# Filter taps of a convolution by distances, two images or four in one operation

## The chip, the cores and the metric

The kernel runs on one core of a Trainium2 chip. The core's engines take part side by side, each with its own instruction stream: TensorE (PE in the profile; its weight loads are shown as PEld) multiplies matrices into PSUM, VectorE (DVE) and ScalarE (ACT) do elementwise work, GpSimd (POOL) does little here, and SyncE (SP) issues most DMAs. The metric is the time of one execution in device microseconds; lower is better.

## The reference, cut to what matters

Sixteen images of 128 channels and 28 x 28 places go through four layers. Layer 0, which the change touches, is an "adder" convolution: each output is minus a sum of absolute differences over channels and nine taps, not a sum of products.

```python
x = x + L0(group_norm(x))     # L0: -sum over 128 channels, 9 taps of |w - x|; 128 filters, 3x3, zero padding
x = L1(x)                     # two 3x3 convolutions with 4-bit weights, batch norm, quantized
t = tokens(x)                 # 784 tokens of 128 channels per image
t = t + additive_attention(ln(t))   # scores[i, j] = v . tanh(Wi[i] + Wi[j]), softmax over j
t = t + mixture_of_experts(ln(t))   # 8 experts, the best 2 per token
t = t + linear_attention(ln(t))
t = t + spectral(ln(t))             # 16 causal filters as products with banded matrices, and more
```

Everything is float32.

## The kernel before, in words

**Layer 0 as taps.** `|w - x|` is made in one of two ways. Kind "a": ScalarE writes `|w - x|` in one activation (line 1351). Kind "m": VectorE writes `max(x, w)` (line 1353), since `|w - x| = 2 max(x, w) - x - w`; a second tap of kind "m" may be added onto the first in the same tile (line 1355, `max(x, w) + part`). Each such tile, 128 channels by two images, holds one tap, or two merged ones, of one filter. TensorE then sums it over the channels: the weights are a block of 32 columns that is zero but for one column of -1 or -2 (`sel`, shifted so that the column falls on the filter's row), and the matmul adds into that filter's row of a PSUM accumulator (line 1335). A matmul with 32 weight columns uses one of TensorE's four column groups. The parts `-x` and `-w` of kind "m", and what taps outside the image bring, are added by `plain_taps` (one small product per pair) and as a bias `sw`.

**Tiling.** The images go in eight pairs. A pair has its input in `pad`, rows of the two images alternating, with a border of zeros. Each of the four column groups has its quarter of the filters, 32, and a list of the tiles of these filters in order; a `Plan` says which taps are kind "a", kind "m", or merged ("m45" are taps 4 and 5 in one tile). One step (`streams`) takes the next tile of each of the four lists, shifted against each other by `turns`, so that a step mixes both kinds: four tiles, then 16 matmuls (four tiles by four PSUM banks of 14 interleaved rows, 392 columns). Pair 0 has the plan ALONE (264 steps), pair 1 SECOND (256), pairs 2 to 7 BESIDE (208 each, 6.5 tiles per filter).

**Order around it.** All else is interleaved with these steps by hand. In step n (loop at line 1360) the code emits, in this order: `rows` (score units: four tanh of 394 columns on ScalarE, line 917, whose products for TensorE wait in `products`, line 901); `taps_of(n + 1)`; the next elementwise parts of the lanes (`ahead`); `sums(n)`, the step's 16 matmuls; the products; the next TensorE parts of the lanes (`behind`). The lanes are generators that yield `EV` before elementwise work and `PE` before TensorE work: `plain` (plain_taps), `convs` (group norm of the next pair and the quantized convolutions of the last, line 542), `conv_out` (the spectral layer: per job three 128-wide matmuls u at line 1232, a copy on ScalarE at line 1242, one 128-wide product into out at line 1235, and band and mat fetches on SP's queue at lines 1179 and 1181, two jobs ahead), and `chain` (the token layers). A rate per lane says how many parts a step takes. TensorE keeps the order as emitted; the other engines' orders are a scheduler's.

**Buffers.** Tap tiles rotate through a ring of ten, shared with other short-lived tiles (`slot`); in pair 0 there are more places. At a pair's end the convolutions must be through, `pad` is rewritten (line 488), and VectorE adds accumulators, bias and the pair's input into `x1p` (line 1385, eight operations of 196 columns). After pair 7 comes the tail: score units that are left (in a form with the adds on VectorE, line 910, and one tanh for four rows, line 912), the rest of the chain and the spectral layer.

Of the kernel before, what the change touches and what calls it, by code (L numbers as in the profile page):

```python
# [20 lines left out]
TAPS = [(dy, dx) for dy in range(3) for dx in range(3)]  # L21


class Plan:
# [5 lines left out]
    def __init__(self, kinds, tiles_of, turns, maxima):  # L30
        self.kinds, self.tiles_of, self.turns, self.maxima = kinds, tiles_of, turns, maxima

    def streams(self):


        quarters = []
        for j, turn in enumerate(self.turns):
            mine = [(m, *x) for m in range(32) for x in self.tiles_of(m, j)]
            quarters.append(mine[turn:] + mine[:turn])
        return list(zip(*quarters))  # L40

    def cut(self, kind):


        of = {}
        for j in range(4):
            for m in range(32):
                for x, taps in self.tiles_of(m, j):
                    for k, region in zip(taps, regions(taps)):
                        if x == kind and region != WHOLE:  # L50
                            of.setdefault(k, set()).add(32 * j + m)
        return {k: frozenset(f) for k, f in of.items()}
# [7 lines left out]
def maxima(all_, **some):  # L60
    return [(int(k), "all") for k in all_] + [(int(k), of) for of, taps in some.items() for k in taps]

FOUR, OTHER = tiles("a0 m4 a2 m5 a6 m7 a8 m13"), tiles("a0 m4 m1 a2 m5 m3 a6 m7 m8")
ALONE = Plan("alone", lambda m, j: OTHER if (m + j) % 4 == 3 else FOUR, (0, 2, 5, 7), maxima("13457", fourth="8"))

EARLY = 6
TWO, ONE = tiles("m13 a0 m4 m5 m6 a2 m7 m8"), tiles("m13 a0 m4 m5 m6 m2 m7 m8")
SECOND = Plan("second", lambda m, j: FOUR if m < EARLY else ONE if (m - EARLY) % 2 else TWO, (0, 2, 5, 7),  # L70
              maxima("13457", late="68", late_odd="2"))

SIX, SEVEN = tiles("m13 a0 m45 m6 a2 m78"), tiles("m13 a0 m7 m45 a2 m8 m6")
BESIDE = Plan("beside", lambda m, j: SEVEN if (m + j) % 4 > 1 else SIX, (0, 2, 4, 5), maxima("1345786"))
CONV_TAPS = [1, 2, 3, 4, 5, 6, 7]


def reach(k):

    dy, dx = TAPS[k]  # L80
    return 2 * (dy == 0), 2 * HW - 2 * (dy == 2), int(dx == 0), HW - (dx == 2)


WHOLE = reach(4)


def regions(taps):


    first = reach(taps[0])  # L90
    for k in taps[1:]:
        r = reach(k)
        if r[0] < first[0] or r[1] > first[1] or r[2] < first[2] or r[3] > first[3]:
            first = WHOLE
    return [first] + [reach(k) for k in taps[1:]]
# [19 lines left out]
RING, ROWS = 10, 14  # L115


RATE_X, RATE_Y, RATE_S, RATE_C, RATE_A, RATE_0, RATE_T, RATE_Z = 1.2, 0.93, 2.0, 1.0, 1.5, 0.9, 2.0, 0.75
# [89 lines left out]
def kernel(ctx: ExitStack, tc: tile.TileContext, a: dict, out: bass.AP):  # L208
# [5 lines left out]
    ring = ctx.enter_context(tc.tile_pool(name="ring", bufs=RING))  # L214
# [6 lines left out]
    NP = B // 2  # L221


    stage = {"pair": 0, "prepared": False, "alone": False}
    turns = {"psx": 0, "psu": 0, "row": 0, "tap": 0}
# [20 lines left out]
    def tap_slot(name):  # L246
        places = []
        if stage["pair"] == 0:
            places = [rows_in[:, 4 * WIN * k : 4 * WIN * k + 2 * T] for k in range(ROWS // 4)]
            if stage["prepared"]:  # L250
                places += [spare(2 * T) for _ in range(4)]
        k = turns["tap"] = (turns["tap"] + 1) % (RING + len(places))
        return places[k] if k < len(places) else slot(2 * T, name)

    def slot(n, name):
        return ring.tile([P, 4 * WIN], F32, tag="d", name=name)[:, :n]
# [6 lines left out]
    def load_pair(p, name):  # L263
        t = slot(2 * T, name).rearrange("p (b t) -> p b t", b=2)
        nc.sync.dma_start(t, a["x"][2 * p : 2 * p + 2].rearrange("b c t -> c b t"))
        return t
# [10 lines left out]
    x0 = load_pair(0, "x0")  # L277
# [34 lines left out]
    pad = const.tile([P, PR, PC], F32, name="pad")  # L312
    x1p = const.tile([P, PR, PC], F32, name="x1p")
    q1p = const.tile([P, PR, PC], F32, name="q1p")
    for t in (pad, x1p, q1p):
        nc.vector.memset(t, 0.0)


    masks = one.tile([P, NE, P], F32, tag="dg", name="masks")
    nc.vector.memset(masks[:, :3], 0.0)  # L320
    fourth, late, late_odd = (masks[:, i, :] for i in range(3))
    for j in range(4):
        nc.vector.memset(fourth[:, 32 * j + 3 - j : 32 * j + 32 : 4], 1.0)
        nc.vector.memset(late[:, 32 * j + EARLY : 32 * j + 32], 1.0)
        nc.vector.memset(late_odd[:, 32 * j + EARLY + 1 : 32 * j + 32 : 2], 1.0)
    filters = {"all": ones, "fourth": fourth, "late": late, "late_odd": late_odd}

    sw = {}
    for plan in (ALONE, SECOND, BESIDE):
        wsum = one.tile([P, P], F32, tag="gate", name=f"wsum_{plan.kinds}")  # L330
        part = one.tile([P, P], F32, tag="gt", name=f"part_{plan.kinds}")
        nc.vector.memset(wsum, 0.0)
        for k, of in plan.maxima:
            nc.vector.tensor_tensor(part, w0[:, k, :], filters[of], ALU.mult)
            nc.vector.tensor_tensor(wsum, wsum, part, ALU.add)
        q = ps("sw_ps")
        nc.tensor.matmul(q[:, :1], wsum, ones[:, :1], start=True, stop=True)
        sw[plan.kinds] = const.tile([P, 1], F32, name=f"sw_{plan.kinds}")
        nc.vector.tensor_copy(sw[plan.kinds], q[:, :1])

    taken = {}
    NB = len(TAPS)
    for plan in (ALONE, SECOND, BESIDE):
        taken[plan.kinds] = const.tile([NB + len(plan.maxima), P], F32, name=f"taken_{plan.kinds}")
        for i, (_, of) in enumerate(plan.maxima):
            nc.sync.dma_start(taken[plan.kinds][NB + i : NB + i + 1, :], filters[of][:1, :])
    channel_sums = scratch.tile([PR, PC], F32, name="channel_sums")
# [3 lines left out]
    row_sets = slot(12 * P, "row_sets")  # L351

    def row_of(fs):

        if fs not in sets:
            t = sets[fs] = blk(row_sets, len(sets) - 1)
            nc.vector.memset(t[:1], 0.0)
            for j in range(4):
                left = sorted(f - 32 * j for f in fs if f // 32 == j)
                while left:  # L360
                    runs = [[m for m in range(left[0], 32, step)] for step in (1, 2, 4)]
                    runs = [r[: next((i for i, m in enumerate(r) if m not in left), len(r))] for r in runs]
                    run = max(runs, key=len)
                    step = run[1] - run[0] if len(run) > 1 else 1
                    nc.vector.memset(t[:1, 32 * j + run[0] : 32 * j + run[-1] + 1 : step], 1.0)
                    left = [m for m in left if m not in run]
# [161 lines left out]
    def quantized_convs(p):  # L528
        yield EV
        lv = None  # L530
        for i, name, src in ((0, "L1_conv_w1", x1p), (1, "L1_conv_w2", q1p)):
            w = slot(9 * P, f"{name}_{p}").rearrange("p (k f) -> p k f", f=P)
            nc.sync.dma_start(w, wq[name].rearrange("p (k f) -> p k f", f=P))
            if i == 0:
                yield EV
# [894 lines left out]
```

## Time and profile before

| what | value |
|---|---|
| time, median of 3 runs | 11,595.7 us (11,589.33 to 11,598.8) |
| the profiled execution's own time | 11,592.63 us |
| its span | 11,590.9 us |
| busy: PE, DVE, ACT | 10,973.1, 10,499.6, 10,074.4 us |
| tap operations on DVE: L1353, L1355 | 4,493.8 and 3,720.7 us |
| tap operations on ACT: L1351 | 3,233.6 us |
| tanh of scores on ACT: L917 | 5,285.5 us |
| tap matmuls on PE: L1335, both kinds | 5,056.6 and 4,176.8 us |
| mean granted TensorE clock | 0.986 |
| DMA | 393.14 MB, q1 at 11.9% of the 16 engines |

Busy time of PE is the union of matmul records; matmuls overlap, so it says when something was in flight and not how much of PE was used. In a row of an operation, the count after x is followed by its busy time and the mean duration of one in ns, then by the idle time of the engine before it and what ended it. A window's row has, for each engine, busy time and number of instructions, then the TensorE clock, the DMA share and GB/s. The pads' rewrites start at 859, 2,038, 3,332, 4,654, 5,982, 7,328 and 8,665 us, and the last tap matmul ends at 9,992 us; these are the ends of the stages.

### The profile page before, as it was taken

To read this page: it belongs to the slowest core of one execution; us is meant where nothing else is said; L and a number is where in the kernel's file an instruction comes from. 1 tells how busy PE (TensorE), PEld (TensorE's weight loads), DVE (VectorE), ACT (ScalarE), POOL (GpSimd) and SP (SyncE) were. 2 spreads that over 40 slices of the span, in tenths; PEclk is the share of its full clock that TensorE was granted. 3 is DMA by queue.
4 is the path that set the end of the run, shared out by engine and by line. 5 is a ranking of instruction groups with operands and counts; after the bars stand their busy time and mean duration, and the time that the engine had idled before them with its cause. 6 is when DMAs were issued, how large, how long until landed. Compare 5 with 4: busy or idle time off the path is not lost.

```text
span 11590.9 us, 236925 instructions
## 1 busy us (share of the span) xinstructions
PE 10973.1 (95%) x97914; PEld 6520.6 (56%) x97914; DVE 10499.6 (91%) x15188; ACT 10074.4 (87%) x14557; POOL 173.3 (1%) x145
## 2 busy tenths in 40 slices
PE   7999999999999999999999999999999999999999
PEld 5554655565555655555555555565555655444446
DVE  9998899999999999999999899999999999999981
ACT  7887998979989898898988989899798998988872
POOL 0000000000000000000000000000000000000000
PEclk9999999999999999999999999999999999999999
DMA  1210000010110111011010110111110111121224
GB/s 31 62 38 4 1 3 10 17 39 23 38 31 24 39 28 42 19 32 38 26 39 22 33 37 25 30 33 33 37 30 20 36 34 38 33 57 52 57 59 108
DMA packets 417672, 393.14 MB, mean 34 GB/s; under 512 B 48297, under 2 KB 402945, under 8 KB 416338
## 3 DMA queue, kind: packets, MB, share of 16 engines
q1 hardware_dynamic: 416162, 376.23, 11.9%
q8 instruction: 771, 12.63, 0.5%
q14 instruction: 307, 2.51, 0.1%
q10 hardware_dynamic: 432, 1.77, 0.0%
HBM read 359.86 MB, written 17.94 MB: 33 GB/s over the span
## 4 chain that ended last, share of the span: by engine, by line
PE 54%; DVE 20%; ACT 18%; issue 2%; POOL 0%; DMA 0%; ACTq 0%; DVEq 0%; POOLq 0%; SPq 0%
PE acc L1335 22%; ACT rows_in L917 11%; PE sp L901 10%; PE u L1232 10%; DVE d L1353 7%; DVE d L1355 7%; ACT d L1351 5%; PE out L1235 4%; PE conv_ps L542 2%; DVE th L910 2%; PE ex L1070 1%; PE av L985 1%; ACT th L912 1%; DVE mx L961 1%; DVE sc L974 1%
## 5 line engine op out<-in xcount | busy, mean ns | idle before, releaser
L917 ACT ACTIVATE rows_in<-wi 128x394 f32<-128x394 f32 x9872 | 5285.5, 628 | 197.9 <-PE sp L901 191.3
L1335 PE MATMUL acc<-d,sel_m 128*32 128x392 f32 (+3 forms) x37224 | 5056.6, 493 | 127.3 <-DVE d L1355 119.4
L1353 DVE TENSOR_SCALAR d<-pad,w 128x1458 f32<-128x1458 f32 (+2 forms) x4653 | 4493.8, 1005 | 317.4 <-PE acc L1335 312.5
L1335 PE MATMUL acc<-d,sel_a 128*32 128x378 f32 (+1 forms) x17136 | 4176.8, 479 | 70.2 <-ACT d L1351 69.1
L1355 DVE SCALAR_TENSOR_TENSOR d<-pad,w,d 128x1512 f32<-128x1512 f32 (+1 forms) x2113 | 3720.7, 1778 | 8.5
L1351 ACT ACTIVATE d<-pad,w 128x1458 f32<-128x1458 f32 x2142 | 3233.6, 1537 | 372.3 <-PE acc L1335 365.3
L1335 PEld LDWEIGHTS acc<-d,sel_m 128*32 128x32 f32 x37224 | 1927.5, 111 | 927.3 <-issue 419.6
L901 PE MATMUL sp<-rows_in,vz 128*32 128x394 f32 x19744 | 2275.8, 496 | 0.8 <-ACT rows_in L917 0.8
L1335 PEld LDWEIGHTS acc<-d,sel_a 128*32 128x32 f32 x17136 | 1380.7, 111 | 1097.9 <-issue 292.4
L1232 PE MATMUL u<-band,up 128*128 128x392 f32 (+2 forms) x6144 | 1626.7, 401 | 19.1 <-ACT us L1242 15.9
L1232 PEld LDWEIGHTS u<-band,up 128*128 128x128 f32 x6144 | 1093.1, 190 | 958.6 <-issue 243.1
L901 PEld LDWEIGHTS sp<-rows_in,vz 128*32 128x32 f32 x19744 | 1270.6, 110 | 475.1 <-ACT rows_in L917 107.2
L912 ACT ACTIVATE th<-th 128x1576 f32<-128x1576 f32 x668 | 980.5, 1529 | 110.3 <-DVE th L910 104.0
L910 DVE TENSOR_SCALAR th<-wi 128x394 f32<-128x394 f32 x2672 | 933.6, 422 | 3.4 <-PE sp L901 2.7
L901 PE MATMUL sp<-th,vz 128*32 128x394 f32 x5344 | 532.1, 506 | 75.0 <-ACT th L912 73.9
L1235 PE MATMUL out<-us,mat 128*128 128x392 f32 (+1 forms) x1408 | 580.4, 494 | 0.1
L1242 ACT COPY us<-u 128x392 f32<-128x392 f32 x704 | 337.3, 479 | 235.0 <-PE u L1232 233.2
L1242 ACT COPY rows_in<-u 128x392 f32<-128x392 f32 x320 | 154.3, 482 | 280.1 <-PE u L1232 279.4
L1074 DVE SCALAR_TENSOR_TENSOR t<-ex,gate,t 128x128 f32<-128x128 f32 x896 | 309.1, 347 | 51.7 <-PE ex L1070 45.0
L901 PEld LDWEIGHTS sp<-th,vz 128*32 128x32 f32 x5344 | 132.7, 109 | 367.1 <-ACT th L912 202.5
L1070 PE MATMUL ex<-ew,xt 128*128 128x512 f32 x448 | 235.9, 610 | 41.1 <-DVE t L1074 37.7
L1235 PE MATMUL out<-rows_in,mat 128*128 128x392 f32 (+1 forms) x640 | 261.3, 493 | 0.0
(318 smaller groups left out, 5947.8 us busy)
## 6 DMA issues: line engine op xcount, KB each, us to landing
band<-band SPq DMA_DIRECT2D x1024, 196.0 KB
mat<-mats SPq DMA_DIRECT2D x1024, 64.0 KB
lags<-lag_mats SPq DMA_DIRECT2D x80, 192.0 KB
L_conv_w<-q_L_conv_w SPq DMA_DIRECT2D x16, 576.0 KB
ew<-in_L_ffn_expert_w_dram SPq DMA_DIRECT2D x16, 512.0 KB
eb<-eb_rows SPq DMA_DIRECT2D x16, 448.0 KB
x<-in_x_dram SPq DMA_DIRECT2D x8, 784.0 KB
band<-band_out SPq DMA_DIRECT2D x32, 196.0 KB
```

The costliest lines, as they stand in the source:

```text
L901: nc.tensor.matmul(sp[32 * j : 32 * j + 32, lo : lo + WIN], vz[:, 32 - m : 64 - m], rows[j], start=m == 0, stop=m == Q - 1, skip_group_che ...
L910: nc.vector.tensor_scalar(th[:, j, :], wi[:, i + Q * j : i + Q * j + WIN], wi[:, i + Q * j : i + Q * j + 1], None, ALU.add)
L912: nc.scalar.activation(th, th, AF.Tanh)
L917: nc.scalar.activation(rows[j], wi[:, i + Q * j : i + Q * j + WIN], AF.Tanh, bias=wi[:, i + Q * j : i + Q * j + 1])
L1070: nc.tensor.matmul(q, blk(xt, i), ew[:, 4 * h : 4 * h + 4, :], start=True, stop=True)
L1232: nc.tensor.matmul(q[:, P * i : TH], up[:, to ^ odd, i, :], t[:, :w], start=i == 0, stop=i == 2)
L1235: nc.tensor.matmul(acc[:, lag:TH], m0, u[:, : TH - lag], start=False, stop=n is None and not copied)
L1242: nc.scalar.copy(u[:, :TH], q[:, :TH])
L1335: nc.tensor.matmul(acc[:, lo - 14 * c : hi - 14 * c, c0:c1], sel[kind][:, 31 - m : 63 - m], d[:, lo:hi, c0:c1], start=n == 0, stop=n == le ...
L1351: nc.scalar.activation(part, x, AF.Abs, bias=wk, scale=-1.0)
L1353: nc.vector.tensor_scalar(part, x, wk, None, ALU.max)
L1355: nc.vector.scalar_tensor_tensor(part, x, wk, part, ALU.max, ALU.add)
```

## The change

The images are taken in five groups: images 0-1, then 2-5, 6-9, 10-13 (four at a time), then 14-15. A tap tile of a group of four is 128 channels by four images, and one operation writes it. TensorE's four column groups become the four images: a tile's eight matmuls (four images by two PSUM banks of 14 rows) all use the same weights. With four images, an accumulator of two banks holds 32 filters, so a group goes through the filters in four phases; groups of two images take two tiles per step and two phases. Accumulators exist twice and phases take turns. The input has no border now; taps only write the places that they reach, and merged taps are chosen so that the first covers the second. At a phase's end ScalarE adds the bias and writes the sums to DRAM (`x1s`), and the quantized convolutions read them back with the input. Plans per group are new, tap operations are emitted two (half as large) steps ahead and not one, rates are per group, and the ring of ten tiles becomes ten half tiles with explicit owners (`take`, `free`; `lend` for other users, four at most). `ROWS` goes from 14 to 12.

```diff
+class Group:
+    def __init__(self, first, n, plan, rows, pace):
+        self.first, self.n, self.plan, self.rows, self.pace = first, n, plan, rows, pace
+        self.tall = n * HW
+    def firsts(self, phase):
+        return [P // self.n * phase + 32 * (j // self.n) for j in range(4)]
+    def streams(self, phase):
+        lists = []
+        for f0 in self.firsts(phase)[:: self.n]:
+            mine = [(f0 + m, *x) for m in range(32) for x in self.plan.tiles_of(f0 + m)]
+            turn = self.plan.turn if lists else 0
+            lists.append(mine[turn:] + mine[:turn])
+        return list(zip(*lists, strict=True))
...
-SIX, SEVEN = tiles("m13 a0 m45 m6 a2 m78"), tiles("m13 a0 m7 m45 a2 m8 m6")
-BESIDE = Plan("beside", lambda m, j: SEVEN if (m + j) % 4 > 1 else SIX, (0, 2, 4, 5), maxima("1345786"))
+FOUR, OTHER = tiles("a0 m4 a2 m5 a1 m7 a8 m36"), tiles("a0 m4 m1 a2 m5 m3 a6 m7 m8")
+ALONE = Plan("alone", lambda f: OTHER if (f + f // 32) % 4 == 3 else FOUR, 5)
+SEVEN, EIGHT = tiles("a0 m45 a2 m1 a6 m78 m3"), tiles("a0 m4 a2 m5 m1 a6 m78 m3")
+EARLY = Plan("early", lambda f: EIGHT if f % 2 else SEVEN)
+TWO, THREE = tiles("a0 m45 m1 a2 m78 m6 m3"), tiles("a0 m45 m1 m36 m2 m78")
+BESIDE = Plan("beside", lambda f: THREE if f % 4 == 3 else TWO)
+ONE, NONE = tiles("a0 m45 m1 m78 m2 m36"), tiles("m0 m45 m1 m78 m2 m6 m3")
+LATE = Plan("late", lambda f: NONE if (f + f // 32) % 2 else ONE, 3)
+GROUPS = (Group(0, 2, ALONE, 0.0, 1.0), Group(2, 4, EARLY, 0.85, 0.9), Group(6, 4, BESIDE, 1.95, 1.0),
+          Group(10, 4, BESIDE, 1.95, 1.0), Group(14, 2, LATE, 3.2, 1.6))
...
-RING, ROWS = 10, 14
+HALVES, HALF, ROWS = 10, 2 * T, 12
+AHEAD = 2
+STEP = 208
...
+    def tap_sums_out(g, phase, accs):
+        s = take(1)
+        if s is None:
+            return False
+        t = s.ap[:, :T]
+        for c in range(2):
+            nc.scalar.activation(t[:, c * NCK : (c + 1) * NCK], accs[c][:, :NCK], AF.Identity,
+                                 bias=sw[g.plan.name][:, phase : phase + 1])
+        for j, f0 in enumerate(g.firsts(phase)):
+            nc.sync.dma_start(x1s[g][j % g.n, f0 : f0 + 32, :], t[32 * j : 32 * j + 32])
+        s.free()
+        return True
...
-    def quantized_convs(p):
+    def quantized_convs(g, p):
+        held = None
+        while held is None:
+            yield EV
+            held = lend(2)
+        first, raw = (held.ap[:, i * HALF : (i + 1) * HALF].rearrange("p (b t) -> p b t", b=2) for i in range(2))
+        lo = 2 * p - g.first
+        nc.sync.dma_start(raw, a["x"][2 * p : 2 * p + 2].rearrange("b c t -> c b t"))
+        nc.sync.dma_start(first, x1s[g][lo : lo + 2].rearrange("b c t -> c b t"))
+        for _ in range(3):
+            yield EV
+        for im in range(2):
+            nc.vector.tensor_tensor(own(x1p, im, 0, HW), first[:, im, :].rearrange("p (h w) -> p h w", w=HW),
+                                    raw[:, im, :].rearrange("p (h w) -> p h w", w=HW), ALU.add)
...
+    def taps_of(k):
...
+        for f, kind, taps in stream:
+            s = take(n // 2)
+            d = s.ap.rearrange("p (r w) -> p r w", w=HW)
+            for at, tap in enumerate(taps):
+                (dy, dx), (r0, r1, c0, c1) = TAPS[tap], reach(tap)
+                part = d[:, n * r0 : n * r1, c0:c1]
+                x = rows_of_input(g)[:, n * (r0 + dy - 1) : n * (r1 + dy - 1), c0 + dx - 1 : c1 + dx - 1]
...
+    def sums(k, accs, first, last):
+        g = GROUPS[seq[k][0]]
+        for c in range(2):
+            for j in range(4):
+                _, d, m, kind, (r0, r1, c0, c1) = made[k][j // g.n]
+                lo, hi = max(r0, 14 * c), min(r1, 14 * c + 14)
+                nc.tensor.matmul(
+                    in_rows(accs[c][32 * j : 32 * j + 32, :NCK])[:, lo - 14 * c : hi - 14 * c, c0:c1],
+                    sel[kind][:, 31 - m : 63 - m],
+                    d.rearrange("p (h b) w -> p h b w", b=g.n)[:, lo:hi, j % g.n, c0:c1],
+                    start=first, stop=last, skip_group_check=True,
+                )
+        for s, *_ in made.pop(k):
+            s.free()
...
+            pace["rows"] = STEP * g.n / 2 / length
+            pace["by"] = pace["rows"] * g.pace
...
+        rows(g.rows)
+        while emitted < min(k + AHEAD + 1, len(seq)):
...
+            taps_of(emitted)
+            emitted += 1
+        if outs and outs[0][0] <= k and tap_sums_out(*outs[0][1:]):
+            _, done, part, _ = outs.pop(0)
+            if part + 1 == done.n:
+                convs.add(*(quantized_convs(done, p) for p in range(done.first // 2, (done.first + done.n) // 2)))
+        ns = ahead()
+        sums(k, accs, first, last)
```

## The prediction

> **What bounds it now.** I read the totals first, then the busy time by stage, then the rows of the tap operations, then short timelines, then the waits.
>
> ```profile
> PE 10973.1 (95%) x97914; PEld 6520.6 (56%) x97914; DVE 10499.6 (91%) x15188; ACT 10074.4 (87%) x14557; POOL 173.3 (1%) x145
> ...
> 859.00:2038.00 1179.00, 1074.04 (x11261) 665.87 (x11257) 1035.22 (x1250) 1025.08 (x1538) 16.55 (x7) 0.98 0.02 5
> 4654.00:5982.00 1328.00, 1278.98 (x11480) 770.78 (x11482) 1234.02 (x1495) 1220.10 (x1945) 15.67 (x11) 0.99 0.12 31
> 9992.00:11591.00 1599.00, 1498.13 (x9780) 784.63 (x9772) 1233.29 (x3924) 1165.90 (x1149) 25.79 (x20) 0.99 0.23 62
> ```
>
> The last three lines are pair 1, pair 4 and the tail (after the last tap matmul, at 9,992 us); their columns are length, then busy time of PE, PEld, DVE, ACT. In the tap stages three engines are all over 90% busy, so a saving on one is worth only what the other two allow. For PE the busy column says too much, because matmuls overlap. Its real price is in start times:
>
> ```profile
> 745.54 0.49 PE L1335 MATMUL acc<-rows_in,sel_m 128*32 128x392 f32 x1
> 745.87 0.49 PE L1335 MATMUL acc<-rows_in,sel_m 128*32 128x392 f32 x1
> 746.20 0.49 PE L1335 MATMUL acc<-rows_in,sel_m 128*32 128x392 f32 x1
> ...
> 5003.09 1.69 PE L901 MATMUL sp<-rows_in,vz 128*32 128x394 f32 x16
> 5004.71 1.60 PE L1232 MATMUL u<-band,up 128*128 128x392 f32 x6
> 5006.15 0.82 PE L1235 MATMUL out<-us,mat 128*128 128x392 f32 x2
> 5006.90 0.51 PE L1335 MATMUL acc<-d,sel_m 128*32 128x378 f32 x1
> ```
>
> Each column group takes a 392-column pass every 0.33 us, so 1.2 columns per ns, four groups side by side. Each matmul of the code leaves two records (two passes). The 16 sp records need 16 x 394 / 4 / 1.2 = 1.31 us, but u starts 1.62 us later: going from 32-wide to 128-wide matmuls costs 0.29 us (the middle of 584 such places is 294 ns). u to out costs 0.12 (1.44 against 1.32), and back to 32-wide 0.10 (0.75 against 0.65). Columns plus these switches I call PE's need. It is 10,562 us for the whole program: 9,811 of columns, 629 of 1,610 switches at 0.39, 123 of 1,024 u-to-out steps.
>
> ```profile
> 4100.00:4200.00 100.00, 100.00 (x896) 62.24 (x892) 89.21 (x97) 95.64 (x158) 1.48 (x1) 1.00 0.15 39
> 8900.00:9000.00 100.00, 88.45 (x743) 53.40 (x741) 99.52 (x119) 56.74 (x74) 0.00 (x0) 0.97 0.10 28
> ```
>
> In the first of these stretches PE's need is 100 us of 100, in the second 85 while VectorE is full: the bound changes hands every few steps, by what the lanes put in. The waits of 2,038 to 9,990 us agree, tap operations waiting for the matmuls that free their buffers:
>
> ```profile
> ACT d L1351 <- PE acc L1335: 259.0, 119, 12.6
> DVE d L1353 <- PE acc L1335: 192.7, 165, 6.0
> ```
>
> **The change, part by part.** *Wider operations.* Their price, by rows of the same operation in different sizes:
>
> ```profile
> L1353 DVE TENSOR_SCALAR d<-pad,w 128x1568 f32<-128x1568 f32 x1953 | 1983.9, 1030 | 137.8 <-PE acc L1335 134.1 <-ACT rows_in L917 1.2 <-issue 0.2
> L910 DVE TENSOR_SCALAR th<-wi 128x394 f32<-128x394 f32 x2672 | 933.6, 422 | 3.4 <-PE sp L901 2.7 <-ACT th L912 0.6
> L1355 DVE SCALAR_TENSOR_TENSOR d<-pad,w,d 128x1512 f32<-128x1512 f32 x1729 | 3071.7, 1788 | 7.1
> L1351 ACT ACTIVATE d<-pad,w 128x1458 f32<-128x1458 f32 x2142 | 3233.6, 1537 | 372.3 <-PE acc L1335 365.3 <-DMA which_beside<-ones 2.3 <-DVE pad L488 1.5
> ...
> 5009.02 3.71 DVE L1353 TENSOR_SCALAR d<-pad,w 128x1458 f32<-128x1458 f32 x4
> ```
>
> 1,174 more elements cost 608 ns: 0.52 ns per element and 218 fixed. Of the fixed part some 85 ns lie under the next operation (four 1,458s in a row take 3.71 us, 0.89 from start to start where each lasts 0.97), so an operation less saves 130 ns. SCALAR_TENSOR_TENSOR has 1.04 ns per element and the same 130. On ScalarE a 1,458 follows another after 1.43 us; at 0.83 ns per element (activations of 448 and 336 elements last 661 and 569 ns) that leaves 211 fixed.
>
> By the order of the instructions, VectorE's tap operations go from 6,948 (4,804 TENSOR_SCALAR, 2,144 SCALAR_TENSOR_TENSOR) to 4,384 (3,200 and 1,184), of which 2,624 serve four images. Fixed part: 2,564 x 0.130 = -333 us. The new plans merge fewer taps: 360,000 elements more at 0.52 (+188) and 333,000 fewer at 1.04 (-347). Together -493. ScalarE's go from 2,268 to 1,376: 892 x 0.211 = -188, and 82,000 elements at 0.83 fewer, -69; together -257. The rest: 74 score units move from the beside stages into the tail, each four adds of 0.33 on VectorE (+99) and an activation of 1.41 for four of 0.52 on ScalarE (-48); the x1 spill replaces 64 operations of 0.33 by 16 of about 0.9 (VectorE -7) and adds 32 activations of 0.52 on ScalarE. Sums: VectorE 10,359 to 9,950 us, ScalarE 9,949 to 9,660.
>
> [...]
>
> *TensorE.* Fewer merged taps mean more tap tiles: 28,288 matmuls become 29,056, and 277,952 more columns in two passes over four groups at 1.2 per ns are +116 us. A step is now half as large (8 matmuls, not 16; 864 steps for four images, not 416), and the lanes put their 128-wide matmuls into more of these smaller steps: 1,870 switches instead of 1,610, +101 us at 0.39. PE's need rises from 10,562 to 10,778 us. An image's rows now lie four apart in the tile; records of 14 pieces of 27 cost per column what the unbroken 392 cost, so I take nothing for that.
>
> [...]
>
> *Pair changes.* The pad is rewritten seven times, with VectorE waiting at most 1.8 us before each; now four times, with accumulators in two sets. -10 us at most.
>
> *Transfers.* The x1 spill is 12.8 MB on top of 393 at a 12% DMA share; nothing for bandwidth. On SP's queue its writes wait for ScalarE, and behind them stand band fetches, which come two jobs ahead (some 13 us). Nothing if a hold stays below that; 16 holds of 5 us too long would be 80. A read back that lands late would hold VectorE, eight times; the same few us each.
>
> **The sum.** A total by engine is no answer where the bound changes hands. So I cut each program's order into stretches of steps and charge each stretch its busiest engine. For the kernel before, stretches of 8 steps (some 50 us) give 827 us for pair 0, 1,136 for pair 1, 7,946 for pairs 2 to 7 and 1,510 for the tail (PE's need): 11,419. Measured: 859, 1,178, 7,954, 1,599. What is missing (32, 42, 8, 89: start, first scores, pair changes, the last image's chain), 171 us, brings 11,590, the span of 11,590.9. I keep 171 for the new kernel and use stretches of the same work, 16 of its steps:
>
> ```
>                         PE need    VectorE    ScalarE    stretches
> images 0-1                  705        783        709          823
> images 2-5                1,640      1,702      1,712        1,872
> images 6-9                2,511      2,323      2,264        2,657
> images 10-13              2,560      2,320      2,281        2,683
> images 14-15              1,725      1,483      1,424        1,789
> tail                      1,637      1,339      1,271        1,637
> ```
>
> 11,461 + 171 - 10 = 11,622; the own time of the profiled run (11,592.6) is 1.7 over its span, so **11,625 us**, 0.3% over that run and over the median of 11,595.7. VectorE and ScalarE get 4% and 3% faster and TensorE, with 2% more to do, becomes the bound in about two thirds of the stretches from image 6 on: the gain is lost there.
>
> **Rivals.** *TensorE runs closer to its need (not slower).* With 8 to 10% of slack on the other two in images 6 to 13, and buffers freed tile by tile, engines may smooth over twice as far, 32 steps. Those stretches give 813, 1,848, 2,602, 2,636, 1,765, 1,637, so 11,301 + 171 = 11,470. For it: PE's need is 100% of several 100-us stretches today. Against: in the tail, where the others are a quarter idle, PE's need is 94% of the time. It decides if images 6 to 13 take under 5,290 us.
>
> *The half step is too short a cushion (clearly slower).* One tile is all on ScalarE or all on VectorE (a merged one some 5 us of VectorE against 3.1 us for a step), operations are emitted two half steps ahead, and a lane's matmul at the end of a step stands behind them. If engines then smooth over 8 half steps only, the stretches give 11,662 + 171 = 11,833; late SP holds would look alike and add at most 100. It decides if PE's waits for d grow although VectorE is less busy.
>
> *The wide operation isn't cheaper:* if a four-image operation costs two of the old, VectorE keeps the 333 us and ScalarE the 188. In images 6 to 9 VectorE then has 2,323 + 928 x 0.13 = 2,444 us to TensorE's 2,511, and with no slack left the time ends near the second rival's.
>
> **Chances.** Forecast 0.42 (11,550 to 11,700), first rival 0.34 (11,350 to 11,550), second and third 0.24 (11,700 to 11,900). A measurement tells 0.2% from no change, so 11,572 to 11,619 is the same: 0.12, out of the forecast's case, which puts 0.06 below and 0.24 above. Faster 0.06 + 0.34 = 0.40; slower 0.24 + 0.24 = 0.48. The range leaves a tenth off each end of these cases: 11,400 to 11,830.
>
> **What would show it.** Four-image TENSOR_SCALAR of 3,136 at 1.85 us, SCALAR_TENSOR_TENSOR of 3,024 at 3.37, ScalarE's 2,916 at 2.75; VectorE's busy time down by some 400, ScalarE's by 290; tap records of L1457 with unchanged starts 0.33 us apart; images 6 to 9 and 10 to 13 at some 2,650 to 2,680 each, the tail at 1,725. It is wrong if the tap operations scale otherwise, if PE idles for d in the middle stages, or if VectorE or SP waits at the x1 spill.

## The result and the profile after

The changed kernel takes 11,784.78 us (median of 4 runs, 11,781.99 to 11,793.19), the kernel before on the same chip 11,597.25 us (4 runs): 187.5 us more, ratio 1.0164, 95% interval [1.0146, 1.0181]. The forecast was 11,625 us, 0.3% slower; so its sign held and its size did not. In what follows, "over" is a kernel's median less that of the kernel before on the same chip (the change: 187.5), and times of stages are those of the profiled execution (span 11,791.4 us, own time 11,793.19).

The page's totals of the changed kernel, and the windows of its stages from images 2-5 to the tail (bounds and length, then busy time of PE, PEld, DVE, ACT, POOL, then TensorE's clock):

```profile
PE 11008.6 (93%) x99720; PEld 4985.0 (42%) x99720; DVE 10167.6 (86%) x12868; ACT 9795.4 (83%) x13475; POOL 185.9 (2%) x142
```

```profile
846.90:2807.60 1960.70, 1741.13 (x18817) 711.41 (x18817) 1737.95 (x1150) 1721.68 (x1754) 16.01 (x8) 0.96 0.04 10
2807.60:5552.10 2744.50, 2566.38 (x23310) 1112.21 (x23314) 2376.98 (x2122) 2287.10 (x3554) 35.60 (x19) 0.97 0.10 29
5552.10:8286.80 2734.70, 2584.64 (x23612) 1137.93 (x23608) 2369.53 (x2095) 2310.50 (x3600) 40.52 (x20) 0.98 0.11 32
8286.80:10058.20 1771.40, 1740.74 (x14610) 838.58 (x14605) 1530.23 (x2102) 1481.95 (x2791) 25.97 (x15) 1.00 0.14 40
10058.20:11791.40 1733.20, 1625.30 (x10658) 843.85 (x10647) 1356.13 (x4295) 1283.00 (x1251) 29.13 (x22) 0.98 0.22 62
```

VectorE is 332 us less busy than before and ScalarE 279, as the change meant. TensorE is busy 35 us more and the span is 200 us longer: most of the loss, 165 us, is time in which nothing ran on TensorE. Images 6 to 13, where the other chains run beside the taps, show it best (before in the first fence, after in the second):

```profile
3332.40:8664.60 5332.20, 5111.32 (x45755) 3082.38 (x45747) 4965.68 (x6009) 4818.20 (x7646) 74.33 (x41) 0.99 0.12 31
```

```profile
2807.60:8286.80 5479.20, 5151.03 (x46918) 2250.14 (x46922) 4746.51 (x4217) 4597.59 (x7154) 76.12 (x39) 0.97 0.11 30
```

They take 147 us more; TensorE's idle time rose from 221 to 328 us, while VectorE and ScalarE got 219 and 221 us less to do. The waits of these stages, first of before, then of after, say who waits for whom:

```profile
DVE d L1353 <- PE acc L1335: 143.9, 116, 6.0
...
PE acc L1335 <- DVE d L1355: 44.9, 47, 2.7
PE nu L1123 <- DVE t L1140: 27.2, 13, 4.6
PE ex L1070 <- DVE t L1074: 22.5, 16, 3.7
```

```profile
DVE work L1446 <- PE acc L1457: 460.8, 254, 6.6
...
PE ex L1174 <- DVE t L1178: 72.9, 27, 7.6
PE acc L1457 <- DVE work L1446: 46.0, 7, 10.7
PE nu L1227 <- DVE t L1244: 43.8, 17, 5.3
PE acc L1457 <- DVE work L1448: 29.7, 22, 4.6
```

VectorE waits three times as long for TensorE to free a tile's place, and TensorE waits longer for VectorE, above all with matmuls that are not taps: all waits of PE for VectorE ahead of such matmuls add up to 121 us before and 219 us after, those ahead of tap matmuls to 45 and 76. (In images 2 to 5 it is the other way round: the former fell from 70 to 53 us, the latter rose from 39 to 152.) VectorE has less to do, TensorE's busy time is hardly longer, and yet they wait more for each other: that points to order and latency rather than to work. One such place, VectorE first, then PE:

```profile
3318.51 0.35 DVE L1178 SCALAR_TENSOR_TENSOR t<-ex,gate,t 128x128 f32<-128x128 f32 x1
3318.77 3.25 DVE L1448 SCALAR_TENSOR_TENSOR work<-work,w 128x2916 f32<-128x2916 f32 x1
3321.93 0.35 DVE L1178 SCALAR_TENSOR_TENSOR t<-ex,gate,t 128x128 f32<-128x128 f32 x1
3322.19 1.84 DVE L1446 TENSOR_SCALAR work<-work,w 128x3136 f32<-128x3136 f32 x1
3323.95 0.34 DVE L1178 SCALAR_TENSOR_TENSOR t<-ex,gate,t 128x128 f32<-128x128 f32 x1
3324.21 3.36 DVE L1448 SCALAR_TENSOR_TENSOR work<-work,w 128x3024 f32<-128x3024 f32 x1
3327.49 0.35 DVE L1178 SCALAR_TENSOR_TENSOR t<-ex,gate,t 128x128 f32<-128x128 f32 x1
```

```profile
3320.90 0.84 PE L1005 MATMUL sp<-rows_in,vz 128*32 128x394 f32 x8
3327.98 1.19 PE L1174 MATMUL ex<-ew,xt 128*128 128x512 f32 x1 [6.23 <-DVE t L1178]
```

An expert's product `ex` is added to `t` by four chained operations of 0.35 us, and the next `ex` needs that PSUM bank again. Between the four stand three tap operations of up to 3.36 us, so they take 9.3 us, and TensorE, whose order is fixed, stands for 6.23 us. I counted these fours in images 6 to 13: before, 108 of them took 5.9 us at most; after, 22 of 98 took over 6 us. The long ones are new, but the mean didn't rise: 3.5 us before and 3.3 after, since only 46 of the 98 have something in between. A step lasted 6.4 us before (5,332 us in 832 steps); a half step now lasts 3.2 (5,479 in 1,728), so a four can now span three turns.

### The profile page after: what moved, and what is told of

It reads as the page before. It is cut to its first block, busy times and chain, and to the rows that moved or that the text cites. A ratio compares the mean times of both kernels' runs of the same rounds, so it can differ in the third digit from the quotient of the medians.

```text
span 11791.4 us, 237615 instructions
## 1 busy us (share of the span) xinstructions
PE 11008.6 (93%) x99720; PEld 4985.0 (42%) x99720; DVE 10167.6 (86%) x12868; ACT 9795.4 (83%) x13475; POOL 185.9 (2%) x142
## 4 chain that ended last, share of the span: by engine, by line
PE 64%; DVE 25%; ACT 7%; issue 3%; POOL 0%; DMA 0%; SPq 0%; DVEq 0%; ACTq 0%; POOLq 0%
PE acc L1457 26%; PE sp L1005 12%; PE u L1336 11%; DVE work L1446 10%; DVE work L1448 8%; PE out L1339 5%; ACT rows_in L1021 4%; DVE work L1014 3%; PE conv_ps L645 3%; ACT work L1444 2%; PE ex L1174 2%; PE av L1089 1%; DVE t L1178 1%; DVE rows_in L1446 0%; ACT work L1016 0%
## 5 line engine op out<-in xcount | busy, mean ns | idle before, releaser
L1446 DVE TENSOR_SCALAR work<-work,w 128x3024 f32<-128x3024 f32 (+5 forms) x3050 | 4444.7, 1484 | 841.4 <-PE acc L1457 797.6
L1457 PE MATMUL acc<-work,sel_m 128*32 128x392 f32 (+3 forms) x39248 | 3905.2, 495 | 254.2 <-DVE work L1448 197.5
L1444 ACT ACTIVATE work<-work,w 128x2916 f32<-128x2916 f32 (+2 forms) x1242 | 2872.9, 2331 | 633.8 <-PE acc L1457 578.7
L1448 DVE SCALAR_TENSOR_TENSOR work<-work,w 128x2916 f32<-128x2916 f32 (+3 forms) x1154 | 3202.2, 2780 | 11.0
L1457 PEld LDWEIGHTS acc<-work,sel_m 128*32 128x32 f32 x39248 | 1257.2, 111 | 2223.7 <-issue 1677.0
L1457 PE MATMUL acc<-work,sel_a 128*32 128x351 f32 (+2 forms) x16592 | 1742.4, 480 | 29.3 <-ACT work L1444 29.2
L1016 ACT ACTIVATE work<-work 128x1576 f32<-128x1576 f32 x742 | 1089.2, 1522 | 112.1 <-DVE work L1014 107.7
L1014 DVE TENSOR_SCALAR work<-wi 128x394 f32<-128x394 f32 x2968 | 1039.1, 420 | 6.2 <-PE sp L1005 3.2
L1457 PEld LDWEIGHTS acc<-work,sel_a 128*32 128x32 f32 x16592 | 593.5, 111 | 773.2 <-issue 667.9
L1005 PE MATMUL sp<-work,vz 128*32 128x394 f32 x5936 | 591.7, 508 | 70.2 <-ACT work L1016 69.8
```

The costliest lines, as they stand in the source:

```text
L1005: nc.tensor.matmul(sp[32 * j : 32 * j + 32, lo : lo + WIN], vz[:, 32 - m : 64 - m], rows[j], start=m == 0, stop=m == Q - 1, skip_group_che ...
L1014: nc.vector.tensor_scalar(th[:, j, :], wi[:, i + Q * j : i + Q * j + WIN], wi[:, i + Q * j : i + Q * j + 1], None, ALU.add)
L1016: nc.scalar.activation(th, th, AF.Tanh)
L1444: nc.scalar.activation(part, x, AF.Abs, bias=wk, scale=-1.0)
L1446: nc.vector.tensor_scalar(part, x, wk, None, ALU.max)
L1448: nc.vector.scalar_tensor_tensor(part, x, wk, part, ALU.max, ALU.add)
```

## The theories

- **TensorE's need.** The 768 tap matmuls and 260 switches more raised TensorE's need by 216 us (10,562 to 10,778), and time followed: time over need is 1.097 before and 1.094 after.
- **Short cushion.** The second rival of the prediction: tap tiles come too late for a half step.
- **Long operations in the way.** Short steps of other chains stand behind tap operations twice as long, and TensorE waits for them.
- **Ring.** Five places of four images make VectorE and TensorE wait for each other.

## The experiments

Lengths of stages in us, from the trace of one execution of each (images 2-5 of the kernel before are its pairs 1 and 2):

```
                                   0-1     2-5    6-13   14-15    tail    over
before                             859   2,473   5,332   1,327   1,599       0
after                              847   1,961   5,479   1,771   1,733     188
e1 TensorE's work less             846   1,956   5,389   1,771   1,730     107
e2 VectorE's work less             846   1,959   5,440   1,771   1,735     164
e3 rarer turns                     843   1,960   5,266   1,766   1,868     115
e4 split by height                 846   1,959   5,393   1,775   1,733     118
e4c split by columns               846   1,989   5,422   1,773   1,734     174
e5 VectorE in emitted order        921   1,912   5,409   1,805   2,032     488
e13 the same in images 2-13        847   1,918   5,412   1,771   1,733      86
e7b three half steps ahead         843   1,966   5,505   1,782   1,732     236
e11 six places, 4 rows             838   1,937   6,189   2,023   1,721   1,122
e6 8 rows                          842   1,968   5,511   1,818   1,741     287
e12 = e13 + e4 + e3                846   1,952   5,290   1,765   1,867     130
e14 before with 12 rows            858   2,490   5,342   1,334   1,607      39
```

**e1, e2: whose work is the bound?** Images 6 to 13 with less for one engine.

```diff
-        for c in range(2):
+        left_out = seq[k][0] in (2, 3) and seq[k][2][0][2] == (3,)
+        for c in range(0 if left_out else 2):
```

> Leaves out, for images 6 to 13, TensorE's tap matmuls of the tile m3 of 96 filters in each of the two groups (so part of the filters' sums is missing); VectorE and ScalarE still make every tile, and buffers come free at the same half steps. That is 192 tiles of 8 matmuls, which take 1.3 us a tile in the trace after the change: 250 us less for TensorE, and nothing less for another engine. Theory of TensorE's need: the changed kernel lost 188 us because the tap matmuls and switches added 216 us to TensorE's need, and time follows that need (11,590/10,562 = 1.097 before, 11,791/10,778 = 1.094 after); then 250 us come off, times 1.09 at most: 11,510 to 11,540 us. Theory of the short cushion (the second rival: half steps of 3.4-us operations make TensorE wait for VectorE's and ScalarE's tiles and for the experts' short steps that stand behind them): TensorE's idle time grows by most of what is taken away, and less than half of it comes off: 11,660 to 11,760 us.

```diff
+                if i in (2, 3) and at == 1 and tap == 5 and f % 10 < 3:
+                    continue
```

> Leaves out, for images 6 to 13, VectorE's second tap of the tile m45 of 39 filters in each of the two groups (so those filters lack one maximum); TensorE's matmuls and ScalarE are as they were. That is 78 operations of 3.3 us, 256 us less for VectorE. Theory of TensorE's need: VectorE is 86% busy and not the bound, the need of TensorE is unchanged: 11,750 to 11,790 us. Theory of the short cushion: VectorE's work is what TensorE waits for in images 6 to 13, in half steps that the cushion does not even out, so at least half of the 256 us comes off there: 11,530 to 11,660 us.

e1: 11,695.43 us, ratio 1.0092 [1.0075, 1.0108]: 80 of 250 us came off. e2: 11,751.98 us, 1.0139 [1.0124, 1.0154]: 24 of 256. The windows of images 6 to 13, e1 first:

```profile
2802.00:8190.80 5388.80, 4989.56 (x43830) 2185.71 (x43834) 4747.68 (x4223) 4589.53 (x7151) 81.85 (x39) 0.97 0.11 31
```

```profile
2805.40:8245.60 5440.20, 5140.75 (x46918) 2250.72 (x46922) 4501.75 (x4140) 4596.91 (x7154) 68.77 (x39) 0.98 0.11 31
```

e2's wait of VectorE for freed places in the same window (time, how often, longest):

```profile
DVE work L1448 <- PE acc L1459: 598.5, 297, 8.0
```

In e1 TensorE's idle time rose from 328 to 399 us. In e2 VectorE was busy 245 us less and waited 138 us more for freed places (598.5 against 460.8); the intervals hardly tell its 24 us from nothing. So neither engine's work is the bound by itself. As the whole cause TensorE's need falls: it had e2 right, but in e1 all of the 250 us should have come off. That time over need stayed constant was a coincidence. e2 also went against the short cushion, which expected half of the 256 us.

**e3: rarer turns.**

```diff
-        ns = ahead()
+        if g.n == 4:
+            by = pace["by"]
+            pace["by"] = 2 * by * (k % 2)
+            ns = ahead()
+            pace["by"] = by
+        else:
+            ns = ahead()
```

> In the four-image groups the other chains (attention, experts, quantized convolution, output) get their turn only in every second half step, at double the rate, as in the kernel before, where a turn came once per whole step; the tap work is unchanged. Theory of TensorE's need: of the 260 switches that the change added (101 us) about half to all go, 50 to 100 us come off: 11,680 to 11,735 us. Theory of the short cushion: the turns get longer and rarer, so a chain's next short step waits as long as before or longer, and TensorE has more foreign matmuls in a row ahead of the tap matmuls of one half step, that is 0 to 100 us more: 11,785 to 11,885 us.

11,703.68 us, ratio 1.0097 [1.0082, 1.0112]: 72 us off. The switches in the trace fell from 1,870 to 1,663; at 0.39 us that is 81. Images 6 to 13 gained 213 us and the tail lost 135, since fewer parts of the other chains ran beside the taps. The time is what the theory of the need expected and agrees with the prediction's price of a switch, but it doesn't prove that price: TensorE is busy 57 us less and idle 31 us less, and its waits for VectorE ahead of other chains' matmuls fell too, from 219 to 185 us in images 6 to 13. Part of the 72 us may be these waits.

**e4, e4c: the width undone.** Each tap operation of a four-image group becomes two, of half the height (e4) or half the columns (e4c). The core of e4, then of e4c:

```diff
+                tall = n * (r1 - r0)
+                for lo in range(0, tall, tall // (n // 2)):
+                    part, x = (t[:, lo : lo + tall // (n // 2)] for t in (whole_part, whole_x))
```

```diff
+                wide = c1 - c0
+                for lo, hi in ((0, wide // 2), (wide // 2, wide)) if n == 4 else ((0, wide),):
+                    p, v = part[:, :, lo:hi], x[:, :, lo:hi]
```

> Undoes one part: in the four-image groups each tap operation on VectorE and ScalarE is cut into two of half the height, so the wide operation's saving is given back (VectorE about +333 us, ScalarE about +188 us by the two rows of each form), while tiles, phases, buffers, order and TensorE's matmuls stay. The longest tap operation falls from 3.4 to 1.75 us. Theory of TensorE's need: need is unchanged; VectorE at about 10,500 us is as busy as in the kernel before: 11,785 to 11,900 us. Theory of the short cushion in its form that the long operations hold up the experts' and attention's short steps on VectorE and ScalarE: in spite of more work it gets faster, 11,600 to 11,740 us. If the wide operation's saving was worth its full busy time, 12,000 us or more.

> Like the split of e4, but each tap operation of a four-image group is cut by columns, not by height: the same number of operations and elements, but both halves of TensorE's matmuls need both parts, so TensorE can't begin on half a tile. If e4's 78 us came from shorter operations in the way of other chains' short steps: the same here, 11,690 to 11,730 us. If they came from TensorE beginning on the first half of a tile: none of it is left and the added fixed cost shows, 11,785 to 11,900 us.

e4: 11,706.56 us, ratio 1.0101 [1.0086, 1.0116]. The work came back and the time fell by 69 us. Its totals, then waits in images 6 to 13:

```profile
PE 11068.3 (95%) x99720; PEld 5121.6 (44%) x99720; DVE 10439.7 (89%) x15492; ACT 9937.4 (85%) x14307; POOL 179.2 (2%) x142
```

```profile
DVE work L1449 <- PE acc L1460: 265.9, 153, 5.9
...
PE ex L1174 <- DVE t L1178: 47.7, 25, 4.8
```

VectorE is busy 272 us more than in the changed kernel and ScalarE 142, yet it waits for 195 us less and `ex` for 25 less; no four of the experts takes over 5.6 us. TensorE's waits for VectorE ahead of all other chains' matmuls, 219 us in the changed kernel, are 170 in e4 and in e4c: that much of them goes with the length of the tap operations. (In images 2 to 5 the waits ahead of tap matmuls fall from 152 to 41 us in e4 and the stage is 2 us shorter, so there they cost little.) e4c: 11,765.05 us, 1.0151 [1.0134, 1.0168], 14 us off, which its interval doesn't tell from nothing; its value lies between what the two readings expected. It has the same shorter operations, its longest four is 5.4 us, and images 6 to 13 take 57 us less (e4: 86); but images 2 to 5 take 28 more, and ScalarE is busy 60 us more than in e4 (9,997.2). So part of e4's gain is the shorter operation and part is the direction of the cut. In images 6 to 13 the traces lean to TensorE's start on half a tile: ahead of tap matmuls it waits 58 us for VectorE in e4 and 83 in e4c, and 1 and 2 us for ScalarE. In images 2 to 5, where ScalarE holds up tap matmuls for 12 us in e4 and 32 in e4c, the price of narrow pieces on ScalarE may add to it; this is not settled.

**e5, e13: VectorE in the order of the program.** e5 orders all of VectorE's work, e13 only that of images 2 to 13 (`starts` holds where each group begins).

```diff
-    in_traced_order(tc, (mybir.EngineType.PE,))
+    in_traced_order(tc, (mybir.EngineType.PE, mybir.EngineType.DVE))
```

> After the first four runs (a fifth of TensorE's tap matmuls taken away in images 6 to 13 gave less than half back, VectorE's work taken away gave almost nothing, the split operations and the rarer turns each gave some 80 us). This run keeps VectorE's instructions in the order in which the program emits them, as TensorE's already are, so that the four chained accumulations of the experts (L1178, 0.35 us each) stand together and no tap operation of up to 3.4 us gets between them. Theory of the long operations in the way (a short step of another chain stands behind a 3.4-us operation, and TensorE, in order, waits for it): 60 to 150 us less than the changed kernel, 11,635 to 11,725 us, and TensorE's waits for t ahead of ex fall from 96 us to less than 40. Theory of the ring (VectorE and TensorE wait for each other by way of five tile places, whatever the order): no gain, 11,770 us or more, and more if the fixed order makes VectorE stand behind a step that isn't ready.

```diff
     in_traced_order(tc, (mybir.EngineType.PE,))
+    in_traced_order(tc, (mybir.EngineType.DVE,), (starts[1], starts[4]))
```

> VectorE is kept in the order in which the program emits its work only while images 2 to 13 have their turn (e5 kept it in that order everywhere: images 2 to 13 took 118 us less, the first stage 74 us more, the last two 333 us more). Theory of the long operations in the way of the experts' chained steps: the 118 us remain without the loss elsewhere, 11,650 to 11,690 us, with TensorE's wait for t ahead of ex at half of the changed kernel's in images 6 to 13 (73 us). Rival: what e5 won there was lent by the later stages (work of the other chains put off), then the last two stages are longer than 3,505 us by as much and the time is 11,760 us or more.

e5: 12,078.93 us, ratio 1.0421 [1.0406, 1.0437]: a miss as a whole, because the tail alone lost 299 us to the fixed order; but images 2 to 13 took 118 less. e13 keeps nearly all of that (111): 11,677.89 us, 1.0071 [1.0054, 1.0088], 101 us off, the later stages unchanged, as the long operations expected and the loan didn't. VectorE of e13 and its waits in images 6 to 13:

```profile
3270.98 1.50 DVE L1178 SCALAR_TENSOR_TENSOR t<-ex,gate,t 128x128 f32<-128x128 f32 x4
3272.40 1.79 DVE L1446 TENSOR_SCALAR work<-work,w 128x3024 f32<-128x3024 f32 x1
3274.22 3.25 DVE L1448 SCALAR_TENSOR_TENSOR work<-work,w 128x2916 f32<-128x2916 f32 x1
3277.40 1.73 DVE L1446 TENSOR_SCALAR work<-work,w 128x2916 f32<-128x2916 f32 x1
3279.05 1.50 DVE L1178 SCALAR_TENSOR_TENSOR t<-ex,gate,t 128x128 f32<-128x128 f32 x4
```

```profile
DVE work L1446 <- PE acc L1457: 158.2, 95, 6.2
DVE sc L1032 <- PE sp L1005: 113.3, 34, 10.3
...
PE acc L1457 <- DVE work L1448: 72.7, 42, 4.7
PE ex L1174 <- DVE t L1178: 29.5, 20, 3.4
```

All fours stand together (1.5 us each), `ex` waits 29.5 us where it waited 72.9, and VectorE's wait for places falls to a third. But all waits of PE for VectorE ahead of other chains' matmuls only fall from 219 to 203 us: other steps now wait (`qk` 36 us for 10, `mb` 35 for 16). So the order as a whole matters; that the experts' fours are the main share is not shown. Nor is it new with the change that a four is torn: before, 90 of 108 were. No run fixes VectorE's order, or makes the turns rarer, in the kernel before; so how much of e13's 101 us and e3's 72 belongs to the change is not shown.

**e7b, e11, e6, e14: cushion, ring, rows.**

```diff
-AHEAD = 2
+AHEAD = 3
```

> The taps are emitted three half steps ahead of the sums in place of two (in the kernel before it was more in time: whole steps of twice the length); the five tile places stay. Theory of the short cushion (tap tiles are asked for too late, so that TensorE catches up with VectorE): 40 to 120 us less than the changed kernel, 11,665 to 11,745 us. Theory of the ring (the places are full, VectorE waits 798 us for TensorE to free them, so asking earlier changes nothing) and theory of the long operations: within 30 us of 11,785 us.

11,827.53 us, ratio 1.0204 [1.0189, 1.0219]: 49 us more, worse than any theory had it. PE's waits ahead of tap matmuls fell from 76 to 26 us in images 6 to 13, those ahead of the other chains' rose from 219 to 284. More cushion for the taps is taken from the chains; as the cause in these images the short cushion falls. (Two half steps of 3.2 us are as long as the one whole step of before, other than the expectation says.)

```diff
-HALVES, HALF, ROWS = 10, 2 * T, 12
+HALVES, HALF, ROWS = 12, 2 * T, 4
```

> Six tile places of four images in place of five; the room is taken from the rows that hold the transposed copies on their way (12 to 4), so the last stretch, where these rows are used most, may be longer: it is read by stage. Theory of the ring: images 6 to 13, 5,479 us in the changed kernel, take 80 to 200 us less, and VectorE's wait for TensorE ahead of a new tile falls by half. Theory of the long operations: within 30 us of 5,479 us, or longer for want of rows.

12,713.36 us, ratio 1.0970 [1.0953, 1.0986]. It says nothing on the ring: the rows that paid for the sixth place cost far more. TensorE's weight loads for `sp` wait 163.8 us for these rows in images 6 to 13 of the changed kernel, and in this run:

```profile
PEld sp L1005 <- ACT rows_in L1021: 1082.0, 2345, 3.2
```

So the number of places stays untested. That five places hold the two engines up whatever the order, as the ring had it, goes against e13, which gained with the same five.

The run put a question that the prediction had not asked: the change itself takes the rows from 14 to 12.

```diff
-HALVES, HALF, ROWS = 10, 2 * T, 12
+HALVES, HALF, ROWS = 10, 2 * T, 8
```

> The row buffers that carry copies from ScalarE back to TensorE (rows_in) go from 12 to 8; everything else is the changed kernel. The change itself took them from 14 to 12, and the run with 4 rows (and six tile places) lost 310 to 380 us in each stage of images 6 to 13, with TensorE's wait for rows_in grown from 164 to over 1,100 us there. If the rows are a cause of the change's loss: losing four more costs at least twice what losing two did, 50 us or more in images 2 to 13, 11,835 us or more. If 12 rows are enough (theory of the long operations): within 20 us of 11,785 us, and the loss with 4 rows is a cliff below 8.

```diff
-RING, ROWS = 10, 14
+RING, ROWS = 10, 12
```

> The kernel before with 12 row buffers in place of 14 and nothing else: that part of the change by itself. The steps from 12 to 8 in the changed kernel cost 93 us, 23 us a row; a ring of three full sets of four (12) may cost less a row than one of two sets. If two rows fewer are a part of the change's loss: at most 46 us, 11,610 to 11,637 us. If not: within 15 us of 11,590 us.

e6: 11,878.52 us, ratio 1.0245 [1.0230, 1.0261], 100 us more than the changed kernel, so rows do cost there. e14: 11,631.51 us, 1.0035 [1.0021, 1.0049]: two rows fewer cost the kernel before 39 us (24 to 57), spread over all stages but the first. ScalarE's wait for `sp` ahead of L917, over the whole run, is 191.3 us in the kernel before, and here:

```profile
ACT rows_in L917 <- PE sp L901: 230.3, 189, 11.5
```

That wait is longer by 39 us too: by the code, a score unit writes four rows in turn, and a row comes round again after three and a half units with 14 of them, after three with 12. So a part of the loss has nothing to do with four images at all. That the first two rows cost the changed kernel as much as the kernel before is an assumption; no run gives them back.

**e12: three together.** The edits of e13, e4 and e3 in one kernel.

> Three edits at once, each of which gave 80 to 118 us by itself: VectorE in emitted order during images 2 to 13, tap operations of four-image groups cut into two of half the height, and turns of the other chains in every second half step at double the rate. If they remove different waits: 11,785 - 118 - 78 - 81 = 11,508 us, below both kernels. Theory of the long operations: the first two remove the same wait (a short step behind a long operation), so together they give little more than one of them: 11,580 to 11,640 us. If the fixed order needs the even turns (long turns in a row on VectorE leave TensorE without tiles): above 11,700 us.

11,721.83 us, ratio 1.0111 [1.0096, 1.0126]: 57 us off, less than e13 alone. Images 6 to 13 take 5,290 us, no less than with rarer turns alone, and the tail has e3's loss (134 us more than in e13). The gains don't add. The time is where the third reading expected it (above 11,700 us), but not for its reason: TensorE's waits for VectorE ahead of tap matmuls are not the long ones (62 us in images 6 to 13, 78 in e13 and 82 in e3), those ahead of the other chains' are the longest, 239 us against 203 in e13 and 185 in e3. VectorE is 94% busy there again (93% in the kernel before), so the split's added work may have met the end of the slack; that is argued, not shown. No version here beats the kernel before.

## Why the prediction was right in sign and short in size

- **Prices of operations: right.** TENSOR_SCALAR of 3,136 took 1,849 ns (1.85 forecast), SCALAR_TENSOR_TENSOR of 3,024 3,364 ns (3.37), the activation of 2,916 2,733 ns (2.75); VectorE 332 us less busy (400), ScalarE 279 (290). The third rival falls. The tap matmuls kept their 0.33 us.
- **TensorE's need: right in size.** By the records it rose by 216 us, as forecast. But a microsecond of it isn't a microsecond of time: of tap matmuls about a third comes through (e1, 80 of 250), of switches at most nearly all (e3, 72 of 81, with shorter waits among them).
- **The step that failed** is the one that says "I keep 171 for the new kernel and use stretches of the same work, 16 of its steps". It let the lighter VectorE and ScalarE even out TensorE's load as far as before, 5,340 us for images 6 to 13; they took 5,479. That is 139 of the 169 us by which the sum fell short of the span (images 2-5, with the 42 of pair 1, 47 more; the other stages 17 less). What an engine has to do says nothing of when its steps come: TensorE's waits for VectorE ahead of the other chains' matmuls went from 121 to 219 us, and shorter operations alone took them to 170 (e4, e4c); with VectorE 86% busy, cutting the operations up took 69 us off the time (e4). That turns twice as frequent let TensorE meet unfinished chains sooner fits e3 (185), but is argued.
- **The second rival** had nearly the time (11,833) and its sign in the profile: VectorE less busy and PE waiting for it more. Its mechanism was only half right. In images 6 to 13 the wait isn't mainly for tap tiles, and emitting them earlier makes it worse (e7b); it is the "lane's matmul at the end of a step" that stands behind the long operations. The late SP holds, which were to look alike, are out: in the whole run TensorE waits 9 us for DMA (5 before), VectorE 18 (9) and ScalarE 17 (9).
- **Not costed at all:** the two rows, 39 us in the kernel before; and the clock, which fell where TensorE waited (0.977 over the run for 0.986, last section).
- **Luck in the sign.** The time is outside the forecast's own case (11,550 to 11,700 us, chance 0.42) and in that of the second and third rivals, given 0.24. Slower had 0.48 and faster 0.40, so that the sign came true says little for the sum.
- **Slips that changed little:** in the prediction's line of pair 1 VectorE and ScalarE are 88% and 87% busy, not over 90%; its terms for VectorE add up to 9,958 us, not 9,950; the sums of the rivals leave out the 10 us of the pair changes.
- **A ledger**, each by its own run: rows 39 (as in the kernel before); 260 switches at e3's 72 us for 207, 90; tap matmuls a third of 116, some 37; the width itself 14 to 69 (e4c, e4), its saved work included. Together 180 to 235 us, for 188 measured. It is an estimate, and that it comes to the measured loss proves little: e12 shows that such parts overlap, and e3's share may hold waits that the width's share holds too.

## What to carry to other kernels

Where several engines are each near 90% busy and one has a fixed order, price a longer operation by the short chained steps that stand behind it, not only by the busy time that it saves; then cut it up or fix its engine's order for that stretch alone, and measure both. Take a little work away from each engine in turn: if none gives back what was taken (here 80 of 250 us of TensorE and 24 of 256 of VectorE came back), much of the time lies in waits, and sums of work will not find it. Go through every buffer count that a change pays with; two rows of fourteen cost the kernel before 39 us, a fifth of this loss.

## What the runs showed of the hardware

TensorE's granted clock fell where it waited: two stretches of 100 us in the changed kernel, one with waits as in the timeline above, one full.

```profile
3300.00:3400.00 100.00, 68.13 (x558) 21.01 (x560) 74.53 (x99) 59.60 (x88) 1.48 (x1) 0.85 0.00 1
...
8400.00:8500.00 100.00, 100.00 (x804) 47.07 (x806) 87.31 (x119) 88.42 (x166) 1.48 (x1) 1.00 0.12 37
```

Over the whole run it is 0.977 where it was 0.986 (e4: 0.983). The clock's records of both kernels hold two values, 1.0 and 0.5. TensorE in the first of these stretches, ahead of a wait and behind it:

```profile
3300.53 1.43 PE L1457 MATMUL acc<-work,sel_m 128*32 128x378 f32 x16
...
3310.24 2.04 PE L1174 MATMUL ex<-ew,xt 128*128 128x512 f32 x2 [7.62 <-DVE t L1178]
3312.22 2.54 PE L1457 MATMUL acc<-work,sel_m 128*32 128x378 f32 x16
```

Sixteen passes of the same shape take 2.54 us instead of 1.43. Over the run, 392-column passes of one column group start 653 ns apart at half clock and 329 at full (medians, the same in the kernel before). TensorE had matmuls in flight at half clock for 279 us in the kernel before and for 420 after; in images 6 to 13 for 121 and 216, in e4 for 141, in e1 for 280. By 653 against 329 up to half of such time is lost, which makes an estimate of at most 70 us for the change, 48 of them in images 6 to 13, and up to 32 of the 170 us that e1 took from TensorE without getting them back. So in these runs a wait was paid a second time in slower matmuls behind it, and the entries of the ledger hold both.

In the first of these stretches of 100 us the clock of 0.85 goes with gaps of 7.62 and 6.23 us between matmuls. Shorter gaps close together go with a lower clock too: in the 5 us ahead of each of the 110 spells at half clock in the changed kernel, the longest time without a matmul in flight is 2.6 us in the middle case, and matmuls were in flight for 46% of the 5 us (median), against 93% of the whole span.
